# A graph network on one core: VectorE in a written-out order, neighbour lists by original node number, sorted slots weighted by ScalarE and summed in one instruction

## The chip, the cores and the metric

The kernel runs on one core of a Trainium2 chip. A core has five engines with a queue each: TensorE (PE; its weight loads are shown apart as PEld), VectorE (DVE), ScalarE (ACT), GpSimd (POOL) and SyncE (SP). Each works through its own instructions in order, and they wait for each other by semaphores. The metric is the device time of one execution in microseconds, the median of three runs. The profile comes from one further execution.

## The reference

There are B = 16 graphs ("entries") of N = 1024 nodes with C = 64 features, and an adjacency in which each node has a handful of neighbours. Four layers follow each other, each with a residual and a layer norm. Layers 2 and 3 do nearly all of the work here, and they are alike:

```python
x = _layernorm(x + _L0_gnn_ref(...))   # tanh MLP of [x, adj @ x]
x = _layernorm(x + _L1_gnn_ref(x, adj))  # (adj / row sums) @ x
x = _layernorm(x + _L2_gnn_ref(...))   # below
x = _layernorm(x + _L3_gnn_ref(...))   # below, with other weights
# layers 2 and 3:
nb = (adj_ > 0) & (~eye)[None]
skip = jnp.where(m > T_THRESH, (m + K_DIL - 1) // K_DIL, 1)
removed = nb & do_dil[..., None] & ((rank + 1) % skip[..., None] == 0)
rem = removed | jnp.swapaxes(removed, 1, 2)
vals = jnp.where(valid[..., None], x[:, None, :, :], big)
sv = jnp.sort(vals, axis=2)
q = gather(lo) * (1.0 - frac) + gather(hi) * frac
agg = agg + wt * q
h = jax.nn.relu(jnp.einsum('bnc,ch->bnh', x + agg, W1) + b1)
y = (jnp.einsum('bnh,ho->bno', h, W2) + b2) * mask[..., None]
```

In words: a node with more than ten neighbours loses every so many-th of them (and the loss is made symmetric). Then for each node and each feature the values of the remaining neighbours and of the node itself are sorted, and a weighted mean of the three quartiles is taken. A two-layer perceptron and a layer norm follow.

## The kernel before

For each entry there is a preparation and then two sorting phases, one for layer 2 ("layer 0" in the code's `quantiles`) and one for layer 3.

**Preparation** (`prepare`). The adjacency comes in by halves of 2 MB through a single buffer `adj_h`, twice: once for layer 0 (when `near`, the 0/1 matrix of neighbours, is taken from it) and once for layer 1. Then the lists are made. TensorE counts neighbours and their running ranks (`pr`, L458); ScalarE finds by two passes with Sign where a neighbour is to be dropped (L462); VectorE turns the places into one-hot rows `takes` (L470, two per tile of 128 rows); TensorE subtracts these and their transposes from `near` (`pv`, L479 to L485), and ScalarE keeps the rest as `left` (L486). The remaining neighbours are counted by TensorE (`pm`, L496), and the nodes are sorted by that count (keys, L497 to L508). `order` (L515) is the permutation matrix, and `down` (L516) the same, scaled by the place. TensorE permutes node data (`ps`, `px`) and the matrix of neighbours, once on each side: `pw` (L556, copied to `part`, L558) and `pk` (L567). VectorE's MAX8 and MATCH_REPLACE8 (L591, L593) read each row's neighbours out of `pk` as row numbers `idx`, by new, sorted node numbers. The features in the new order go to a DRAM table.

Sorted by count, the eight tiles of 128 nodes have 10, 11, 13, 14, 15, 17, 19 and 33 slots at most (`SIZES`).

**Sorting phase** (`quantiles`, one per entry and layer, 32 in all). Tiles are done from the largest down. For the seven smaller ones GpSimd copies the node's own row into slot 0 (L622) and issues one indirect DMA per further slot (L399, 92 gathers per phase, 128 rows of 256 bytes each) into one of four buffers `got`. For the largest tile, VectorE makes a one-hot matrix `hot` per slot (L630) and TensorE picks the rows with 24 matmuls (L395, features split in three bf16 parts); ScalarE copies eight slots at a time (L636). A sorting network of min and max instructions on VectorE (L639, 288 instructions per phase) moves the values between `got` and a second buffer `other`; only the exchanges that the wanted slots need are there. Then VectorE adds up the wanted slots, each times a weight per node (L644 for the first, L646 for each further one: seven slots for most tiles, 21 for the largest). The perceptron `mlp` ends the phase. For the first of the two layers the result is split in three bf16 parts and written to the table of the second; for the last, GpSimd scatters the rows to the output by `out_rows` (L657).

**What sets the order.** `weave` takes steps in turn from the sorting phases of entry k (layer 0) and k - 1 (layer 1) and from the preparation of entry k + 1, by the share of steps done. The framework's scheduler then orders each engine's instructions, VectorE's among them, and each engine keeps that order. GpSimd's gathers wait for a free `got` buffer, that is, for VectorE's last read of the tile that had it; SP's loads of the adjacency wait for `adj_h`. A general path at the end, for graphs with more neighbours than `SIZES` allows, is skipped in these runs.

Of the kernel before, what the change touches and what calls it, by code (L numbers as in the profile page):

```python
# [126 lines left out]
def exchange_plan(n, want, width=60):  # L127
# [50 lines left out]
    at, (_, ops) = min(beam.items(), key=lambda item: item[1][0])  # L178
    return ops, at
# [3 lines left out]
def adj_resnorm_kernel(ctx: ExitStack, tc: tile.TileContext, x, adj_t, nodemask, w01, b01, w02, b02,  # L183
# [7 lines left out]
    s = SimpleNamespace()  # L191

# [8 lines left out]
    minus_b = const.tile([P, P], BF, name="minus_b")  # L201
    nc.vector.tensor_scalar(minus_b, ident, -1.0, None, op0=ALU.mult)
# [11 lines left out]
                   allow_small_or_imprecise_dtypes=True)  # L214
    eps = const.tile([P, 1], F32, name="eps")
# [49 lines left out]
    table = [[dram.tile([N + 1, C], F32, name=f"table{layer}{i}") for i in range(2)] for layer in range(2)]  # L265
# [18 lines left out]
    def layernorm(dst, y):  # L284
        st = s.work.tile([P, 4, NT], F32, name="ln_st")
        nc.vector.reduce_sum(st[:, 0], y, axis=AX.X)
        nc.vector.tensor_scalar(st[:, 1], st[:, 0], 1.0 / C, None, op0=ALU.mult)
        nc.vector.tensor_sub(y, y, st[:, 1, :, None].to_broadcast([P, NT, C]))
        sq = s.work.tile([P, NT, C], F32, name="ln_sq", bufs=1)
        nc.scalar.activation(sq, y, AF.Square)  # L290
        nc.vector.reduce_sum(st[:, 2], sq, axis=AX.X)
        nc.scalar.activation(st[:, 3], st[:, 2], AF.Sqrt, bias=eps, scale=1.0 / C)
        nc.vector.reciprocal(st[:, 0], st[:, 3])
        nc.vector.tensor_mul(dst, y, st[:, 0, :, None].to_broadcast([P, NT, C]))

    def transposed(src, name):

        dst = s.work.tile([C, N], F32, name=name, bufs=1)
# [22 lines left out]
    def layer0(adj_half, x_s, x1):  # L321
# [3 lines left out]
        for h in range(NH):  # L325
            cols = slice(h * HALF, (h + 1) * HALF)
            adj_h = adj_half(h, True)
# [7 lines left out]
            nc.scalar.activation(hid_t[:, cols], ph[:C], AF.Tanh, bias=b01c)  # L335
        pd = s.psum.tile([P, NT, C], F32, name="pd", tag="mm", bufs=4)
        for t in range(NT):
            nc.tensor.matmul(pd[:, t, :], hid_t[:, t * P : (t + 1) * P], w02s, start=True, stop=True)
        y = s.work.tile([P, NT, C], F32, name="y")
        nc.vector.tensor_add(y, pd, x_s)  # L340
        nc.vector.tensor_add(y, y, b02r[:, None, :].to_broadcast([P, NT, C]))
        nc.vector.memset(x1[:, :, C : C + 1], 1.0)
        layernorm(x1[:, :, :C], y)

    def layer1(adj_half, x1, x2):
        y = s.work.tile([P, NT, C], F32, name="y")
        G = NT // 2
        for g in range(2):
            adj_h = adj_half(g, False)
            pa = s.psum.tile([P, G, C + 1], F32, name="pa", tag="mm", bufs=4)  # L350
            for q in range(G):
                for jt in range(NT):
                    nc.tensor.matmul(pa[:, q, :], adj_h[:, jt, q * P : (q + 1) * P], x1[:, jt, :],  # L353
                                     start=jt == 0, stop=jt == NT - 1)
            deg = s.work.tile([P, 2, G], F32, name="deg")
            nc.vector.tensor_scalar(deg[:, 0], pa[:, :, C], 1.0, None, op0=ALU.max)
            nc.vector.reciprocal(deg[:, 1], deg[:, 0])
            nc.vector.tensor_mul(y[:, g * G : (g + 1) * G, :], pa[:, :, :C],
                                 deg[:, 1, :, None].to_broadcast([P, G, C]))
        nc.vector.tensor_add(y, y, x1[:, :, :C])  # L360
        layernorm(x2, y)

    def mlp(xc, agg, mask, weights, dst):
        w1s, b1c, w2s, b2r = weights
        y = s.work.tile([P, NT, C], F32, name="y")
        nc.vector.tensor_add(agg, agg, xc)  # L366
        o_t = transposed(agg, "x_t")
# [9 lines left out]
        nc.vector.tensor_add(y, pd, b2r[:, None, :].to_broadcast([P, NT, C]))  # L377
        nc.vector.tensor_mul(y, y, mask[:, :, None].to_broadcast([P, NT, C]))
        nc.vector.tensor_add(y, y, xc)
        layernorm(dst, y)  # L380

    def split(xc, parts):

        rest = s.work.tile([P, NT, C], F32, name="rest", tag="y")
        nc.scalar.copy(parts[:, :, 0, :], xc)
        nc.vector.tensor_sub(rest, xc, parts[:, :, 0, :])
        nc.scalar.copy(parts[:, :, 1, :], rest)
        nc.vector.tensor_sub(rest, rest, parts[:, :, 1, :])
# [16 lines left out]
    def prepare(b, e):  # L405


# [4 lines left out]
        def adj_half(h, first):  # L412

            adj_h = s.feat.tile([P, NT, HALF], F32, name="adj_h", bufs=1)
            cols = slice(h * HALF, (h + 1) * HALF)
            load_adj(b, adj_h, cols)
            if first:
                nc.vector.tensor_scalar(near[:, :, cols], adj_h, 0.0, None, op0=ALU.is_gt)
            return adj_h

        x1 = s.feat.tile([P, NT, C + 1], F32, name="x1", bufs=1)
        x2 = s.feat.tile([P, NT, C], F32, name="x2", bufs=1)
        layer0(adj_half, x_s, x1)
        flat = near.rearrange("p t n -> p (t n)")
        diag = flat[:, : (NT - 1) * (N + P)].rearrange("p (t n) -> p t n", n=N + P)[:, :, :P]
        nc.vector.tensor_mul(diag, diag, off_diag[:, None, :].to_broadcast([P, NT - 1, P]))
        nc.vector.tensor_mul(flat[:, NT * N - P :], flat[:, NT * N - P :], off_diag)
        yield
        layer1(adj_half, x1, x2)
        x2p = s.feat.tile([P, NT, 3, C], BF, name="x2p", bufs=1)  # L430
        split(x2, x2p)
        yield


        st = s.work.tile([P, 6, NT], F32, name="nb_st", bufs=1)
        half = s.work.tile([P, NT], I32, name="nb_half", bufs=1)
        m, dil, lim, cut_at, gone = st[:, 0], st[:, 1], st[:, 2:4], st[:, 4:6], st[:, 4:6]
# [15 lines left out]
        for t in range(NT):  # L453
# [10 lines left out]
            if t % 2:  # L464
                yield
# [433 lines left out]
```

## Time and profile before

| | |
|---|---|
| time, median of 3 runs | 7654.07 us (7639.69 to 7656.64) |
| profiled execution | 7622.83 us, its span 7621.1 us |
| mean granted TensorE clock | 0.717 |
| GpSimd gathers L399 | 2944, 3098.5 us |
| VectorE exchanges L639 | 9216 in 8 groups, 3642.5 us |
| VectorE weighting L644 and L646 | 2240, 604.7 us |
| TensorE picks for the largest tile L395, `pgk` | 24576 matmuls, 1056.9 us |
| TensorE second permutation L556, `pw` | 2048 matmuls, 468.4 us |

Busy time is the time in which at least one instruction of the group ran, so a group's figure can be less than its count times its mean. The idle time of an engine is put down to what ended it: a producer by line, "remote" for something that the trace does not show on this core, "issue" where nothing that the trace shows was waited for. The windows give, for a stretch of time, the busy us of PE, PEld, DVE, ACT and POOL with the number of instructions in brackets, then the granted TensorE clock, the mean share of the DMA engines and GB/s.

### The profile page before, as it was taken

To read this page: it belongs to the slowest core of one execution; us is meant where nothing else is said; L and a number is where in the kernel's file an instruction comes from. 1 tells how busy PE (TensorE), PEld (TensorE's weight loads), DVE (VectorE), ACT (ScalarE), POOL (GpSimd) and SP (SyncE) were. 2 spreads that over 40 slices of the span, in tenths; PEclk is the share of its full clock that TensorE was granted. 3 is DMA by queue.
4 is the path that set the end of the run, shared out by engine and by line. 5 is a ranking of instruction groups with operands and counts; after the bars stand their busy time and mean duration, and the time that the engine had idled before them with its cause. 6 is when DMAs were issued, how large, how long until landed. Compare 5 with 4: busy or idle time off the path is not lost.

```text
span 7621.1 us, 112178 instructions
## 1 busy us (share of the span) xinstructions
PE 4154.8 (55%) x44488; PEld 2599.1 (34%) x44488; DVE 5224.3 (69%) x15234; ACT 1125.1 (15%) x1728; POOL 3354.9 (44%) x3338
## 2 busy tenths in 40 slices
PE   7565645456464565645556554565645566554122
PEld 4333323234342333424234331433423343332111
DVE  2567667767667696666777667696666876667666
ACT  3021102011020211102011020111202011020000
POOL 0333354543445444453543445344454444544543
PEclk8787767777676777767777667777766777767555
DMA  1202011020201102011020201102011020100000
GB/s 62 59 15 58 15 41 38 16 59 14 62 18 36 40 16 60 17 41 38 16 60 14 61 18 30 46 15 60 18 40 39 15 59 16 50 18 15 18 17 10
DMA packets 224020, 255.27 MB, mean 33 GB/s; under 512 B 108650, under 2 KB 108794, under 8 KB 223482
## 3 DMA queue, kind: packets, MB, share of 16 engines
q0 software_dynamic: 98304, 100.86, 7.0%
q1 hardware_dynamic: 125178, 147.13, 6.2%
q8 instruction: 350, 5.73, 0.3%
q14 instruction: 188, 1.54, 0.1%
HBM read 235.18 MB, written 12.58 MB: 33 GB/s over the span
## 4 chain that ended last, share of the span: by engine, by line
DVE 37%; PE 20%; another core or an unknown queue 19%; issue 9%; ACT 4%; DMA 1%; POOL 1%; SPq 0%; DVEq 0%; POOLq 0%; ACTq 0%
DVE got L639 11%; DVE other L639 10%; PE pgk L395 6%; DVE agg L646 3%; DVE best L591 3%; PE pa L353 3%; DVE hot L630 3%; PE pr L458 2%; DVE less L593 2%; PE pg L330 2%; ACT junk L506 1%; PE pv L482 1%; DMA adj_h<-in_adj_dram 1%; ACT junk L462 1%
## 5 line engine op out<-in xcount | busy, mean ns | idle before, releaser
L399 POOL DMA_INDIRECT got<-table,idx x2944 | 3098.5, 1052 | 983.3 <-issue 885.8
L395 PEld LDWEIGHTS <-hot 128*128 128x128 bf16 x24576 | 894.9, 103 | 558.5 <-issue 445.3
L639 DVE TENSOR_TENSOR other<-got 128x256 f32<-128x256 f32 (+9 forms) x2176 | 896.9, 425 | 71.2 <-issue 17.9
L622 POOL COPY got<-x2s 128x64 f32<-128x64 f32 x128 | 39.9, 315 | 2039.2 <-DVE agg L646 1611.0
L639 DVE TENSOR_TENSOR got<-other 128x256 f32<-128x256 f32 (+8 forms) x1792 | 736.2, 421 | 27.3 <-remote 7.9
L630 DVE TENSOR_SCALAR hot<-place 128x1024 bf16<-128x1024 f16 x1024 | 431.4, 423 | 449.4 <-remote 273.2
L639 DVE TENSOR_TENSOR got<-got 128x64 f32<-128x64 f32 (+8 forms) x1600 | 656.6, 414 | 33.4 <-DVE agg L646 14.0
L395 PE MATMUL pgk<-x2sp,hot 128*128 128x64 bf16 x12288 | 535.8, 203 | 242.7 <-issue 211.1
L567 PE MATMUL pk<-part,order 128*128 128x512 f16 x2048 | 518.4, 413 | 254.6 <-DVE less L593 221.8
L395 PE MATMUL pgk<-x3sp,hot 128*128 128x64 bf16 x12288 | 521.1, 201 | 181.0 <-issue 150.1
L458 PE MATMUL pr<-steps,near 128*128 128x512 bf16 x1536 | 397.9, 417 | 360.0 <-ACT junk L462 359.8
L302 PE MATMUL pt<-ident,agg 128*64 128x128 f32 x256 | 59.4, 411 | 955.0 <-DVE agg L366 913.9
L622 POOL COPY got<-x3s 128x64 f32<-128x64 f32 x128 | 71.9, 568 | 1072.7 <-DVE agg L646 834.5
L556 PE MATMUL pw<-down,left 128*128 128x512 f16 x2048 | 468.4, 387 | 24.6 <-DVE down L516 24.4
L646 DVE SCALAR_TENSOR_TENSOR agg<-got,wts,agg 128x64 f32<-128x64 f32 x1568 | 422.3, 277 | 69.0 <-remote 23.4
L497 DVE TENSOR_SCALAR own<-pm 128x8 f16<-128x8 f32 x16 | 2.8, 173 | 626.7 <-PE pm L496 626.7
L639 DVE TENSOR_TENSOR other<-other 128x64 f32<-128x64 f32 (+9 forms) x1024 | 390.8, 385 | 24.0 <-DVE got L639 7.1
L567 PEld LDWEIGHTS <-order 128*128 128x128 bf16 x2048 | 208.2, 105 | 556.6 <-DVE less L593 255.1
L482 PEld LDWEIGHTS <-takes 128*128 128x128 bf16 x2048 | 169.6, 113 | 631.0 <-issue 519.5
L302 PEld LDWEIGHTS pt<-ident,agg 128*64 128x64 f32 x256 | 39.1, 165 | 974.8 <-DVE agg L366 561.1
L303 ACT COPY x_t<-pt 64x512 f32<-64x512 f32 x96 | 54.1, 585 | 2111.3 <-issue 1152.0
L458 PEld LDWEIGHTS <-near 128*128 128x128 bf16 x1536 | 163.2, 109 | 552.2 <-issue 415.0
(184 smaller groups left out, 6950.9 us busy)
## 6 DMA issues: line engine op xcount, KB each, us to landing
adj_h<-in_adj_dram SPq DMA_DIRECT2D x512, 256.0 KB
got<-table,idx POOLq DMA_INDIRECT x2944
x_s<-in_x_dram SPq DMA_DIRECT2D x16, 256.0 KB
table<-x2s SPq DMA_DIRECT2D x16, 256.0 KB
table<-x3s SPq DMA_DIRECT2D x16, 256.0 KB
out_dram<-x4s,out_rows POOLq DMA_INDIRECT x128
table<-no_row SPq DMA_DIRECT2D x4, 0.2 KB
b02r<-in_L_gnn_b_dram SPq DMA_DIRECT2D x1, 32.0 KB
```

The costliest lines, as they stand in the source:

```text
L330: nc.tensor.matmul(pg[:C], x_s[:, jt, :], adj_h[:, jt, :], start=jt == 0, stop=jt == NT - 1)
L353: nc.tensor.matmul(pa[:, q, :], adj_h[:, jt, q * P : (q + 1) * P], x1[:, jt, :], start=jt == 0, stop=jt == NT - 1)
L395: nc.tensor.matmul(dst, hot[:, c, :], parts[:, c, q, :], start=first and c + q == 0, stop=c == NT - 1 and q == 2)
L399: nc.gpsimd.indirect_dma_start(out=dst, out_offset=None, in_=tab, in_offset=bass.IndirectOffsetOnAxis(ap=rows, axis=0))
L458: nc.tensor.matmul(pr[:, h * HALF : (h + 1) * HALF], near[:, c, t * P : (t + 1) * P], steps[:, N - P + h * HALF - c * P :][:, :HALF], star ...
L482: nc.tensor.matmul(pv[:, it * P : (it + 1) * P], takes[i][:, it, jt * P : (jt + 1) * P], minus_b, start=False, stop=False)
L556: nc.tensor.matmul(pw[:, cols], left[:, c, t * P : (t + 1) * P], down[:, c, cols], start=c == 0, stop=c == NT - 1)
L567: nc.tensor.matmul(pk[:, cols], order[:, c, t * P : (t + 1) * P], part[:, c, cols], start=c == 0, stop=c == NT - 1)
L591: nc.vector.max(best[:, k : k + 8], rest)
L630: nc.vector.tensor_scalar(hot, e.place, float(k), None, op0=ALU.is_equal)
L639: nc.vector.tensor_tensor(cut(pair[to], v, d if is_max else 0), cut(pair[a], v), cut(pair[b_], v, d), op=ALU.max if is_max else ALU.min)
L646: nc.vector.scalar_tensor_tensor(agg[:, t, :], value, wt, agg[:, t, :], op0=ALU.mult, op1=ALU.add)
```

## The change

VectorE's order is no longer the scheduler's. All its instructions of the main part are issued through `dve`, a wrapper that adds up an estimated duration for each (0.13 us and 960 elements per us, four times as many for some 16-bit instructions), and `manual_schedule` keeps them as written. The other engines stay with the scheduler. Every piece of work is a generator that yields a number of microseconds before its next VectorE instruction; the class `Weave` keeps a due time for each by the clock of `dve`. The sorting network of a phase is the base: after each of its instructions `catch_up` steps all pieces that are due.

The work itself changes in these places:

- Slots: ScalarE multiplies each wanted slot by its weight into `prods` (2240 instructions), and VectorE sums them by one `reduce_sum` per tile (256). The exchange plan is now the one with all wanted slots ending in `got`; it has 288 instructions per phase as before, with the same elements.
- The largest tile is filled one phase ahead (`fill`), in two buffers, its slots 3.3 us apart by the clock.
- Lists: `takes` is one tile in place of two, from |slot - mid| = off, with the absolute value on ScalarE; `left` carries N minus the original node number in place of 1, so that the product `order` times `left` gives the lists by original number, and `pw`, `part` and `down` go. Counting what is left moves from TensorE (`pm`) to ScalarE (a Sign pass with a sum).
- Tables are in the original order, three per layer. The first result `x2` goes there directly; the second one is scattered by GpSimd with `rows`, eight indirect DMAs per entry, read back by SP as `x3` and split from there. One of three splits goes.
- Buffers: `y`, the layer norm's statistics and some others are named per chain; `junk` has three buffers, `wts`, `idx` and `none` four, `rows`, `out_rows` and `mask` five.

Where the pieces stand, by the instruction order of VectorE: in a phase one `hot` stands after every 5 to 9 exchanges, the eight `takes` after every 2 to 5, and the seven MAX8 groups of an entry between the last tiles of a phase, the last three of them next to each other.

```diff
+class Metered:
...
+            self.us += 0.13 + size / (3840 if fast else 960)
...
-        nc.vector.tensor_scalar(gone, cut_at, float(N), 0.5, op0=ALU.add, op1=ALU.mult)
-        takes = [s.sets.tile([P, NT, N], BF, name=f"takes{i}", tag=f"set{i + 1}") for i in range(2)]
...
+            if t < NT:
+                dists.append(s.work.tile([P, N], F16, name="dist", tag="junk", bufs=3))
+                nc.scalar.activation(dists[t], slot, AF.Abs, bias=mid[:, t : t + 1])
+            yield 1.5
+            if t >= 2:
+                dve.tensor_scalar(takes[:, t - 2, :], dists[t - 2], off[:, t - 2 : t - 1], None, op0=ALU.is_equal)
...
+                nc.tensor.matmul(pv[:, cols], near[:, c, rows], scaled[:, c, :], start=True, stop=False)
+                nc.tensor.matmul(pv[:, cols], takes[:, c, rows], minus_n, start=False, stop=False)
+                nc.tensor.matmul(pv[:, cols], minus_n, takes[:, t, cols], start=False, stop=True)
+            nc.scalar.activation(left[:, t, :], pv, AF.Relu)
...
-                    nc.tensor.matmul(pw[:, cols], left[:, c, t * P : (t + 1) * P], down[:, c, cols],
-                                     start=c == 0, stop=c == NT - 1)
-            nc.scalar.copy(part[:, t, :], pw)
...
+                dve.tensor_scalar(hot, e.place, float(k), None, op0=ALU.is_equal)
...
+                pick(pg[:, k - g, :], hot, e.parts[layer], whole)
+                yield 3.3
...
+        for i, k in enumerate(want):
+            nc.scalar.activation(prods[:, i, :], got[:, k, :], AF.Copy, scale=e.wts[:, t, k : k + 1])
+        yield 9
+        dve.reduce_sum(agg[:, t, :], prods.rearrange("p k c -> p c k"), axis=AX.X)
...
+        dst, rows = (out_rows_of, e.out_rows) if layer else (table[1][b % 3], e.rows)
...
+            nc.sync.dma_start(x3, dst[:N, :].rearrange("(t p) c -> p t c", p=P))
...
-            for i, k in enumerate(wants[t]):
-                value, wt = pair[at[k]][:, k, :], e.wts[:, t, k : k + 1]
-                if i == 0:
-                    nc.vector.tensor_scalar(agg[:, t, :], value, wt, None, op0=ALU.mult)
-                else:
-                    nc.vector.scalar_tensor_tensor(agg[:, t, :], value, wt, agg[:, t, :], op0=ALU.mult, op1=ALU.add)
...
+            for is_max, d, v, a, b_, to in usual[t]:
+                dve.tensor_tensor(cut(pair[to], v, d if is_max else 0), cut(pair[a], v), cut(pair[b_], v, d),
+                                  op=ALU.max if is_max else ALU.min)
+                yield
+            yield weigh(e, t, got, agg)
...
+        def catch_up(self):
+            while self.works:
+                work = min(self.works, key=lambda w: w[0])
+                if work[0] > self.now():
+                    return
+                self.step(work)
...
+        main.enter_context(tc.manual_schedule(engines={mybir.EngineType.DVE}))
...
+            for new in sort_tiles(b, entries[b], layer, agg):
+                if new:
+                    weave.add(new)
+                weave.catch_up()
+            finishing[b, layer] = weave.add(finish(b, entries[b], layer, agg))
...
+            phase(k, 0, (k - 1, 1))
+            phase(k - 1, 1, (k + 1, 0))
```

A phase first finishes its own fill, then whatever the fill of the following phase needs (the preparation of entry k + 1, or the end of the first layer), starts that fill, and then sorts. Preparations start one after another: that of entry b + 1 when the lists of entry b are made.

## The prediction

> **What bounds the kernel now.** I read the totals of the page first, then what VectorE (DVE) waited for, then the span in windows of 12 and 15 us, then the costliest groups. Totals:
>
> ```profile
> PE 4154.8 (55%) x44488; PEld 2599.1 (34%) x44488; DVE 5224.3 (69%) x15234; ACT 1125.1 (15%) x1728; POOL 3354.9 (44%) x3338
> ```
>
> VectorE is the busiest, and 7621.1 - 5224.3 = 2397 us of the span it stands idle. POOL's figure leaves out the gap after each gather, so the group list is needed:
>
> ```profile
> L399 POOL DMA_INDIRECT got<-table,idx x2944 | 3098.5, 1052 | 983.3 <-issue 885.8
> L622 POOL COPY got<-x2s 128x64 f32<-128x64 f32 x128 | 39.9, 315 | 2039.2 <-DVE agg L646 1611.0
> L646 DVE SCALAR_TENSOR_TENSOR agg<-got,wts,agg 128x64 f32<-128x64 f32 x1568 | 422.3, 277 | 69.0 <-remote 23.4
> ```
>
> A gather holds POOL (3098.5 + 885.8) / 2944 = 1.353 us. There are 32 sorting phases (16 entries, two layers), 92 gathers each. POOL otherwise waits for VectorE to free a gather buffer. So VectorE's work and its idle time set the pace. Its waits, with total, count and longest:
>
> ```profile
> DVE own L497 <- PE pm L496: 626.7, 15, 44.5
> DVE hot L630 <- remote: 273.2, 56, 28.7
> DVE y L377 <- remote: 221.2, 10, 32.7
> DVE hot L630 <- PE pgk L395: 174.7, 125, 8.6
> DVE deg L356 <- PE pa L353: 124.3, 32, 15.2
> ```
>
> Once per entry it stands some 42 us before L497 for TensorE sums that take 1.6 us. The windows tell why (busy us, then instructions, for PE, weight loads, DVE, ACT, POOL):
>
> ```profile
> 3515.00:3527.00 12.00, 6.27 (x48) 3.79 (x46) 11.20 (x39) 1.72 (x2) 9.40 (x11) 0.86 0.16 24
> 3527.00:3539.00 12.00, 2.23 (x8) 0.50 (x8) 1.08 (x5) 0.00 (x0) 9.26 (x10) 0.64 0.13 27
> 3539.00:3551.00 12.00, 3.79 (x17) 1.95 (x17) 0.00 (x0) 1.02 (x1) 9.09 (x12) 0.64 0.17 25
> 3551.00:3563.00 12.00, 1.97 (x5) 0.52 (x5) 0.00 (x0) 0.00 (x0) 6.40 (x7) 0.50 0.11 22
> 3563.00:3575.00 12.00, 7.36 (x94) 5.47 (x93) 3.13 (x14) 3.19 (x4) 0.00 (x0) 0.64 0.00 1
> ```
>
> While gathers run without a break, TensorE falls to single matmuls; the moment they stop, all engines run. It is no data wait, for in the last stage, where VectorE only sorts, the same happens to it:
>
> ```profile
> 7320.00:7335.00 15.00, 0.00 (x0) 0.00 (x0) 14.88 (x55) 0.00 (x0) 11.26 (x10) 0.50 0.10 17
> 7335.00:7350.00 15.00, 0.00 (x0) 0.00 (x0) 14.14 (x45) 0.00 (x0) 10.67 (x13) 0.50 0.11 22
> 7350.00:7365.00 15.00, 0.00 (x0) 0.00 (x0) 13.51 (x49) 0.00 (x0) 11.79 (x13) 0.50 0.13 26
> 7365.00:7380.00 15.00, 0.00 (x0) 0.00 (x0) 5.54 (x19) 0.00 (x0) 11.47 (x14) 0.50 0.17 26
> 7380.00:7395.00 15.00, 0.00 (x0) 0.00 (x0) 4.02 (x13) 0.00 (x0) 11.47 (x14) 0.50 0.14 25
> 7395.00:7410.00 15.00, 0.00 (x0) 0.00 (x0) 3.13 (x10) 0.00 (x0) 11.34 (x13) 0.50 0.14 25
> ```
>
> For 45 us of a burst of gathers it keeps its pace (149 instructions), then drops to 12.7 busy us in 45, a share of 0.28. I read this as instructions that arrive too slowly beside the gathers:
>
> ```profile
> q8 instruction: 350, 5.73, 0.3%
> q14 instruction: 188, 1.54, 0.1%
> ```
>
> [...]
>
> **Idle time by kind.** Waits put down to nothing local, or to TensorE while it crawled (626.7, 273.2, 221.2, and 102.5 + 54.3 + 47.0 + 43.0 + 25.9 from the same list): 1394 us, 43.6 per phase. Plain waits for a producer (174.7, 124.3, and 117.9 for the adjacency, 60.9 and 59.1, 38.2, 35.8, 25.1, 19.1): 655 us, 20.5 per phase. The other 348 us are start, end and crumbs.
>
> **VectorE's work.** Weighting goes: L646 1984 instructions, 422.3 + 117.1 us, and L644 256, 65.3 us, together 604.7. In their place stand 256 sums: 224 over about 7 slots of 64 (448 elements) and 32 over 21 slots (1344). The nearest row, L291, sums 512 elements in 0.681 us; by element 0.60 and 1.79 us, 134 + 57 = 191 us. It reads unit steps and the new sums read with a stride; at half speed they would cost 382. I take 191, as the adds that read strided blocks of `got` (L639) show no slower rate: 128x256 advances in 0.34 us in the timeline, about 960 elements per us after 0.07. Half of `takes` goes (L470, 102.7): 51.3. `down` goes (L516): 69.2. One of three splits goes (10.9 + 11.0): 21.9. Small copies moved to ACT (9 us) pay for new small instructions. The sorting networks keep their 288 instructions and all their elements. Sum: 5224.3 - 604.7 + 191 - 51.3 - 69.2 - 21.9 = 4668 us, 146 per phase.
>
> **The other engines.** POOL keeps 2944 gathers (3984 us) and 256 copies (112) and gets 128 more scatters, since the layer's result is now written by row indices: 256 x (1.103 busy, L657, + 0.3 issue) = 359. Sum 4455 us, 139 per phase: 7 us below VectorE, so no phase can fall much under 146. Gather indices in the original order change no count. ACT gets 2240 scalings of 128x64: between 0.301 us (128x8, L292) and 0.585 (64x512, L303); I take 0.33, nearer the small one: 739 us. With 128 `dist` (1.11) and 128 counting passes (1.31), less `part` (129.5), and one split less (30), it comes to some 2.0 ms, under a third; at 0.585 to 2.6 ms. Seven scalings add 2.3 us between a tile's last exchange and its buffer's release, covered by the three other buffers; uncovered, 224 x 2.3 = 515 us, inside the high end below. In ACT's queue some stand behind copies that wait for TensorE, so a late TensorE now holds gather buffers too. TensorE loses `pw` (468.4) and L496 (31.2), and 3072 small `pv` matmuls at L482's 0.122 us replace 568: about 3460 us, 108 per phase, not the bound. The read-back of `x3` through SP stands before the next adjacency loads, and behind scatters; its user, the second layer's fill, begins a whole phase later. If that cover went, the chain costs about the 12 us that its yield stands for, 16 times: 192 us.
>
> **Idle after.** The laid-down order puts one `hot` between 5 to 9 exchanges and the list pieces between tiles, so a producer's latency mostly lies behind sorting. Of the plain 20.5 us per phase I keep half, 10; bounds 0 and 20.5. For the fetch stall, follow POOL's order: three tiles per phase (12, 10 and 9 gathers) are gathered one by one as a buffer comes free, 12 to 16 us each, too short to hurt. But the three lightest tiles are sorted in 7 to 10 us each by the row's rates (3840 to 5632 elements), quicker than the next phase's 18, 16, 14 and 13 gathers arrive. These 61 run in one burst of 61 x 1.353 = 83 us. VectorE has 45 us at full pace and 38 at 0.28: it loses 38 x 0.72 = 27, say 28 with its copies. Bounds: 0 (the breaks fall so that every burst stays under 45 us) and today's 43.6. Idle: 348 + 32 x (28 + 10) = 1564.
>
> **Sum.** 4668 + 1564 = 6232 us of span. The profiled execution took 7622.8 with a span of 7621.1, and the median is 7654.1, so 33 us are added: 6265 us.
>
> [...]
>
> **Rivals.**
> - Short bursts (chance 0.20, below 5820). [...] Idle 348 + 32 x 10 = 668, time 4668 + 668 + 33 = 5369. For it: the windows keep full pace for 45 us. Against: POOL has 139 of 146 us to work and can hardly pause.
> - The stalls stay (0.17, 6710 to 7640). The order was laid by a clock that knows nothing of fetching, so the idle time of a phase keeps its 64 us: 4668 + 348 + 32 x 64 + 33 = 7097. For it: a fixed queue stops at its first late piece, and `hot` has only three buffers. Against: VectorE was in order before as well.
> - Slower (0.07). Gathers and VectorE take turns: TensorE serves about 200 matmuls of a burst (201 in the 48 us up to 3527), a hot tile needs 24, every exchange behind it waits, and only 45 us per phase overlap. Then a phase lasts 139 + 146 - 45 = 240 us, idle 94: 4668 + 348 + 3008 + 33 = 8057. It turns into a loss from 81 us idle per phase ((7654 - 33 - 5016) / 32). Against: today's idle is 64 with half the gathers already under sorting.
>
> **How the numbers follow.** The forecast (0.55) holds from 24 to 52 us idle per phase, 5817 to 6713. No difference has 0.01. The range takes the first rival and most of the second: 5400 to 6950, with about 0.2 outside. Under 0.2% this kernel's measurement tells nothing. Faster is 0.55 + 0.20 + 0.17 = 0.92, same 0.01, slower 0.07.
>
> **What would show it.** Right: VectorE busy 4.6 to 4.75 ms, the sums 0.6 and 1.8 us each, ACT near 2.0 ms, no 40 us wait at the `own` line, and windows in which TensorE drops to a few matmuls once per phase near its boundary, ending with the burst. Wrong: POOL busy without pause while TensorE runs at full pace (first rival), or VectorE idle over 60 us per phase, at `hot` above all (second). Strided sums of 1.2 us would add 191 us.

## The result, and the profile after

The changed kernel is slower: 7936.2 us (median of 4, 7925.0 to 7941.3) against 7655.4 us (median of 4), a ratio of 1.0368 with a 95% interval of 1.035 to 1.0387. I had forecast 6265 us. The totals of the profiled execution, span 7934.8 us:

```profile
PE 3952.0 (50%) x41672; PEld 2657.4 (33%) x41672; DVE 5239.9 (66%) x12971; ACT 1806.0 (23%) x4256; POOL 3289.3 (41%) x3466
```

VectorE runs 2263 instructions fewer and is busy 15.6 us longer (5224.3 before), and it stands idle 7934.8 - 5239.9 = 2695 us (2397 before). Both halves of my sum failed. What it waits for (engine, line, releaser: us in total, times, longest):

```profile
DVE hot L196 <- remote: 621.4, 85, 27.0
DVE hot L196 <- PE pgk L431: 474.8, 142, 15.2
DVE best L196 <- remote: 363.5, 19, 39.4
DVE agg L196 <- ACT prods L694: 227.9, 16, 25.3
```

The 626.7 us at `own` are gone. In their place VectorE waits 1096 us at `hot`, 34 us in a phase, and 364 us at the list pieces, 19 times for 19 us on average: pieces that now have a fixed place in its row and whose matmuls are late.

The new sums, out of the costliest groups:

```profile
L196 DVE TENSOR_REDUCE agg<-prods 128x64 f32<-128x448 f32 (+2 forms) x224 | 203.4, 908 | 228.1 <-ACT prods L694 227.9
```

0.908 us for 448 elements where I took 0.60. The windows (columns as in the prediction's) show a burst of gathers and its end:

```profile
3732.00:3744.00 12.00, 0.00 (x0) 0.00 (x0) 11.19 (x34) 2.41 (x10) 9.03 (x10) 0.54 0.13 25
3744.00:3756.00 12.00, 5.71 (x16) 1.99 (x16) 11.53 (x20) 1.26 (x5) 9.31 (x11) 0.75 0.17 26
3756.00:3768.00 12.00, 5.31 (x16) 1.92 (x16) 5.76 (x16) 0.35 (x1) 9.25 (x11) 0.68 0.14 26
3768.00:3780.00 12.00, 0.00 (x0) 0.00 (x0) 3.58 (x8) 2.00 (x7) 9.10 (x11) 0.50 0.17 25
3780.00:3792.00 12.00, 5.54 (x16) 1.97 (x16) 1.61 (x2) 0.00 (x0) 9.39 (x11) 0.78 0.16 27
3792.00:3804.00 12.00, 0.00 (x0) 0.00 (x0) 0.00 (x0) 0.00 (x0) 7.58 (x9) 0.50 0.15 25
```

The gathers have run without a gap of 2.5 us since 3724.7; VectorE is down to half its pace 31 us later, not 45. TensorE's 16 matmuls at a time are the sums of the next list piece. They take 5 to 6 us once they start, but they start only when VectorE has made `less`, and the list piece after them starts only when the gathers have ended (at 3802.0), for a reason that the trace does not show:

```profile
3780.29 5.54 PE L608 MATMUL pk<-left,order 128*128 128x512 f16 x16 [18.84 <-DVE less L196]
3806.87 1.23 DVE L196 MAX8 best<-pk 128x8 f32<-128x1024 f32 x1 [24.96 <-remote]
```

Why busy time did not fall is seen in the step from one instruction to the next. Before, from VectorE's timeline (start, duration):

```profile
3470.80 0.68 DVE L294 TENSOR_TENSOR x<-y,ln_st 128x512 f32<-128x512 f32 x1
3471.40 0.88 DVE L639 TENSOR_TENSOR got<-got 128x704 f32<-128x704 f32 x1
3472.20 0.68 DVE L386 TENSOR_TENSOR rest<-x,x2p 128x512 f32<-128x512 f32 x1
3472.80 0.81 DVE L639 TENSOR_TENSOR got<-other,got 128x640 f32<-128x640 f32 x1
```

and after:

```profile
3629.66 0.69 DVE L196 TENSOR_TENSOR other<-got 128x512 f32<-128x512 f32 x1
3630.39 0.69 DVE L196 TENSOR_TENSOR got<-got 128x512 f32<-128x512 f32 x1
3631.00 0.35 DVE L196 TENSOR_TENSOR got<-other 128x192 f32<-128x192 f32 x1
3631.38 0.36 DVE L196 TENSOR_TENSOR other<-other 128x192 f32<-128x192 f32 x1
```

Before, pieces of other work stand between the exchanges, and each instruction starts 0.08 us before the one ahead of it ends (0.60 us after a start of 0.68). After, the maximum at 3630.39 overwrites what the minimum before it reads, and starts 0.04 us after its end: 0.73 us instead of 0.61. Counted over all neighbours in VectorE's trace (its bookkeeping records included, which puts busy 9 to 28 us above the page's figure; an overlap is counted from 20 ns up, and the pairs in the fourth row have a gap between them):

```
                                 before   after   e1     e8     e13
sum of durations, us             6274     5901    5828   5880   5878
pairs that overlap               12351    6872    12042  8630   9574
their overlap, us                1186     794     1231   927    1027
gaps of 20 to 150 ns             3060     6421    1252   4535   3577
busy (union), us                 5252     5257    4760   5097   5017
```

So 373 us of durations went away and 392 us of overlap with them. The columns e1, e8 and e13 belong to the experiments.

### The profile page after: what moved, and what is told of

It is laid out like the page before. It is cut to its first block, busy times and chain, and to the rows that moved or that the text cites. A ratio compares the mean times of both kernels' runs of the same rounds, so it can differ in the third digit from the quotient of the medians.

```text
span 7934.8 us, 107638 instructions
## 1 busy us (share of the span) xinstructions
PE 3952.0 (50%) x41672; PEld 2657.4 (33%) x41672; DVE 5239.9 (66%) x12971; ACT 1806.0 (23%) x4256; POOL 3289.3 (41%) x3466
## 5 line engine op out<-in xcount | busy, mean ns | idle before, releaser
L435 POOL DMA_INDIRECT got<-table,idx x2944 | 2930.9, 996 | 922.4 <-issue 895.7
L431 PEld LDWEIGHTS <-hot 128*128 128x128 bf16 x24576 | 1103.3, 113 | 2049.3 <-issue 884.7
L431 PE MATMUL pgk<-x3p,hot 128*128 128x64 bf16 x12288 | 709.7, 223 | 1118.5 <-issue 461.8
L608 PE MATMUL pk<-left,order 128*128 128x512 f16 x2048 | 656.6, 478 | 821.9 <-DVE less L196 607.2
L196 DVE TENSOR_TENSOR other<-got 128x256 f32<-128x256 f32 (+10 forms) x2080 | 875.6, 435 | 80.1 <-ACT got L683 13.4
L431 PE MATMUL pgk<-x2p,hot 128*128 128x64 bf16 x12288 | 590.1, 208 | 670.6 <-DVE hot L196 362.1
L694 ACT ACTIVATE prods<-got,wts 128x64 f32<-128x64 f32 x1568 | 408.1, 337 | 1485.6 <-issue 822.9
L196 DVE TENSOR_TENSOR got<-got 128x256 f32<-128x256 f32 (+6 forms) x1472 | 635.3, 434 | 98.4 <-remote 30.6
L536 PE MATMUL pv<-scaled,near 128*128 128x128 f16 x1024 | 270.6, 279 | 307.6 <-issue 207.0
L537 PE MATMUL pv<-minus_n,takes 128*128 128x128 bf16 x1024 | 272.0, 280 | 228.6 <-DVE takes L196 119.9
L507 ACT ACTIVATE junk<-pr,nb_st 128x1024 bf16<-128x1024 f32 x256 | 282.5, 1109 | 446.1 <-PE pr L503 169.3
```

What stands on the lines that cost most here:

```text
L196: return call(*args, **kwargs)
L431: nc.tensor.matmul(dst, hot[:, c, :], parts[:, c, q, :], start=first and c + q == 0, stop=c == NT - 1 and q == 2)
L435: nc.gpsimd.indirect_dma_start(out=dst, out_offset=None, in_=tab, in_offset=bass.IndirectOffsetOnAxis(ap=rows, axis=0))
L507: nc.scalar.activation(junk, pr, AF.Sign, bias=lim[:, i, t : t + 1], scale=-1.0, accum_out=cut_at[:, i, t : t + 1])
L536: nc.tensor.matmul(pv[:, cols], near[:, c, rows], scaled[:, c, :], start=True, stop=False)
L537: nc.tensor.matmul(pv[:, cols], takes[:, c, rows], minus_n, start=False, stop=False)
```

## The experiments

The kernel before took 7644 to 7656 us beside the first two groups of runs (e1 to e5; e7 to e9 and m1) and 7756 to 7767 us beside the other two (e10 to e12 and m2; e13), 1.5% more. Ratios are to the kernel before of the same group; a time in us is compared only inside a group.

**e1: the order left to the scheduler.** One line of the changed kernel is taken out:

```
-        main.enter_context(tc.manual_schedule(engines={mybir.EngineType.DVE}))
```

> The changed kernel with only the laid-down order of VectorE taken back: the scheduler orders VectorE again, lists, weighting by ScalarE and the sum in one go stay. Order theory (the fixed order sets dependent instructions next to each other, so each starts after the end of the one before it instead of 0.1 us earlier): VectorE's busy time falls from 5240 us to 4850 or less, the pairs that overlap rise from 6872 to over 9500, time near 7500. Fetch theory (long bursts of gathers keep instructions from arriving, whatever the order): busy time may fall, but the idle time takes it up, time 7700 to 8000. Third view (the order does what it was written for, and it is the list or weighting part that costs): without it the time is over 8000.

7004.4 us, ratio 0.9168 (0.9152 to 0.9183). Its totals:

```profile
span 6946.2 us, 107593 instructions
...
PE 3768.7 (54%) x41672; PEld 2562.4 (37%) x41672; DVE 4750.6 (68%) x12971; ACT 1806.1 (26%) x4256; POOL 3694.5 (53%) x3466
```

The same 12971 instructions cost VectorE 489 us less (4750.6 against 5239.9), with 12042 overlapping pairs, and it is idle 2196 us instead of 2695. The laid-down order alone costs 13% of the time (1.0368 / 0.9168), some 920 us by the medians and 988 by the two profiled executions (that of e1 was the quickest of its five); without it the change is a gain of 8%. The third view fell, and so did the fetch theory's 7700 to 8000; the order theory's 7500 was too careful: as much again comes from idle time. VectorE's idle time before the list pieces (`best`) is 99 us in all where it was 454, and before `hot` 970 where it was 1134.

**e3 and e9: the weighting alone.** e3 is the kernel before with ScalarE's scalings and one sum; they are packed in place in `got`, for want of memory. e9 is e1 with VectorE's weighting put back.

```
# e3                                        # e9
+prods = got[:, : len(want), :]             -nc.scalar.activation(prods[:, i, :], ...)
+nc.scalar.activation(prods[:, i, :], ...)  -dve.reduce_sum(agg[:, t, :], ...)
+nc.vector.reduce_sum(agg[:, t, :], ...)    +dve.scalar_tensor_tensor(agg[:, t, :], value, wt, ...)
```

> The kernel before with the weighting alone changed: exchanges end in the gathered tile, ScalarE scales the wanted slots (packed in place), VectorE sums them in one instruction. My prediction's step: VectorE loses 604.7 us and gains the sums, busy 5224 to about 4900, time about 7300 if idle time stays. Order theory: the weightings stood between dependent exchanges and cost only their step of 0.20 us each, 2240 x 0.2 = 450, less sums of 281, so busy falls by 170 or less, and time by no more than 170 (7480 to 7650). If the hand-over to ScalarE is itself a loss: over 7700.

> The changed kernel with VectorE's order left to the scheduler and the slots weighted by VectorE again (no products on ScalarE, no sums). Only the lists by original numbers and what goes with them (x3 scattered, TensorE's orders, copies on ScalarE) then differ from before. If the weighting by ScalarE is worth its 170 us of busy time: about 7170. If it costs more in waits (326 us at the sums) than it saves, as it did alone in the kernel before: under 6950. By my prediction's own price for the weighting it would be over 7400.

e3: 7777.8 us, ratio 1.0178 (1.016 to 1.0197). VectorE's busy time falls from 5224 to 5039.9, by 184 us, but its idle time rises by 333 us: new waits come in (166 us at the sums for ScalarE, 307 us at `nb_st` for ScalarE's counting passes or for nothing named), while `own` loses 300. So the weighting alone makes the kernel before slower, by less than 2%. e9: 7084.0 us, ratio 0.926 (0.9216 to 0.9303), busy 4903.3. Read against e1, the weighting is worth 153 us of busy time and 1% of the time (0.926 to 0.9168, intervals that do not touch). My price for it was 414 us. The weightings took 0.277 us each, but their step was 0.20, and where exchanges depend on one another they stood in a place that is now empty. e9 also says what the rest is worth: 7.4% for the lists by original numbers, the largest tile filled a phase ahead, the tables and the buffers together, which no run tells apart.

**e8 and e13: the laid-down order with fewer dependent neighbours.** In e8 the exchanges of a tile are put in another valid order, in e13 the heaviest tile's exchanges also alternate with those of the lighter tiles.

```
-    usual = [exchange_plan(k, want) for k, want in zip(SIZES, wants)]
+    usual = [spread(exchange_plan(k, want)) for k, want in zip(SIZES, wants)]
# e13 besides
+        streams = [exchanges([NT - 1]), exchanges(reversed(range(NT - 1)))]
+            for stream in list(streams):
+                    yield next(stream)
```

> The changed kernel, laid-down order kept, but the exchanges inside each tile are put in another order, so that as few as the network allows read or overwrite what the one before them touched: by the plan 99 such neighbours in 288 exchanges a phase instead of 168. Order theory: 69 x 32 = 2208 pairs overlap again at about 0.12 us each, VectorE's busy time falls by some 200 to 265 us from 5240, and the time by as much if the idle time stays, 7680 to 7740. If the lost overlap is not what made VectorE's busy time stay: busy over 5180.

> The laid-down order kept, exchanges spread as in the run e8, and besides the heaviest tile's 66 exchanges alternate one by one with the first 66 of the lighter tiles, which touch other buffers. By the plan some 58 neighbours of 288 in a phase then depend on each other, against 99 in e8 and 168 in the changed kernel. If adjacency is what took the overlap: VectorE's busy time falls below e8's 5097 (union) to about 4950 to 5000, overlapped pairs over 9500; the time by as much where the idle time stays, about 7600 to 7750 on the chip of the first runs. If something else in the laid-down order keeps VectorE busy: 5080 or more.

```profile
span 7849.7 us, 107652 instructions
...
PE 3884.7 (49%) x41672; PEld 2624.2 (33%) x41672; DVE 5079.3 (65%) x12971; ACT 1817.0 (23%) x4256; POOL 3277.6 (42%) x3466
```

That is e8: 7828.7 us, ratio 1.0216 (1.018 to 1.0252). Busy falls by 161 us, idle rises by 75, so the time stays over the 7740 that I expected at most. 1758 pairs more overlap; 161 / 1758 is 0.09 us each, under the 0.12 that I took. e13:

```profile
span 7473.8 us, 107533 instructions
...
PE 3800.1 (51%) x41564; PEld 2567.2 (34%) x41672; DVE 4998.0 (67%) x12971; ACT 1800.2 (24%) x4256; POOL 3525.2 (47%) x3466
```

7451.9 us, ratio 0.9594 (0.9569 to 0.962): still a laid-down order, with the exchanges alone (and with them the start of the lighter tiles' gathers) in another place, 4% faster than before. Busy is 242 us under the changed kernel's; with the bookkeeping records it is 5017 us, 17 over the range that I gave, and 9574 pairs overlap. From the changed kernel over e8 and e13 to e1, busy time falls with each step in the number of overlapping pairs. Two stages of the small kernels below have the pair by itself, without gathers, both with maxima of 128x256 on VectorE (it is the third engine of the first line, stage n of m2, and the first of the second, stage a of m1):

```profile
2010.00:2040.00 30.00, 0.00 (x0) 0.00 (x0) 27.76 (x66) 0.00 (x0) 0.00 (x0) 0.50 0.00 0
30.00:60.00 30.00, 30.00 (x91) 0.00 (x0) 1.00 0.00 0
```

Where each maximum overwrites what the one before it made, 66 start in 30 us, one in 0.46 us; where none depends on its neighbour 91 do, one in 0.335 us. The granted clock differs, but it is TensorE's, and at 1900 to 1930 us, with 0.92 granted, VectorE's figures in n are the same 27.76 (x66). So it is shown that neighbours that depend on each other took the overlap. In e13 the time fell by more than the busy time; two rows of work also leave a late piece more cover, but that was not tried by itself.

**e7 and e10: half the gathers.** Every second slot is filled by a copy from the slot beside it, so other rows are sorted; in the scheduler's order (e7) and in the laid-down one (e10).

```
-                for k in range(1, size):
+                for k in range(1, size, 2):
                     gather(got[:, k, :], tab, e.idx[:, t, k - 1 : k])
+                nc.gpsimd.tensor_copy(got[:, 2 : 2 * n + 1 : 2, :], got[:, 1 : 2 * n : 2, :])
```

> The changed kernel with VectorE's order left to the scheduler, and every second gather left out (its slot is filled by a copy on GpSimd from the slot beside it, so other rows are sorted): 1472 fewer gathers, some 2 ms less of GpSimd. All the other work is the same. Fetch theory: VectorE's idle time falls from 2196 us to 1300 or less, time under 6250. If the idle time is plain latency between engines (TensorE too slow at its granted clock, hand-overs with ScalarE): idle stays over 1900, time over 6650.

> The changed kernel, laid-down order kept, with every second gather left out and its slot filled by a copy on GpSimd, as in the run with half the gathers in the scheduler's order (5558 us, 770 us of idle on VectorE). If the laid-down order costs only the overlap of dependent instructions: busy 5250, idle near 790, time near 6050. If its fixed places cost waits of their own, gathers or not: idle over 1200, time over 6450. In both cases the idle time beyond that (2695 now) is the gathers'.

The totals of e7, then of e10:

```profile
span 5556.1 us, 106804 instructions
...
PE 3475.2 (63%) x41672; PEld 2450.2 (44%) x41672; DVE 4765.5 (86%) x12971; ACT 1802.8 (32%) x4256; POOL 2428.3 (44%) x2250
```

```profile
span 6130.2 us, 106766 instructions
...
PE 3682.8 (60%) x41575; PEld 2586.4 (42%) x41672; DVE 5256.4 (86%) x12971; ACT 1810.4 (30%) x4256; POOL 2049.8 (33%) x2250
```

5557.8 us and 6131.9 us, one run each. 1504 gathers are left, so 1440 are gone and not the 1472 of the expectation. VectorE's idle time is 791 us in e7 and 874 in e10, where it was 2196 and 2695. So 1440 gathers fewer take away 1405 us of idle time in the one order, 0.98 us for each gather, and 1821 us in the other. With half the gathers the laid-down order costs its 491 us of busy time (5256.4 - 4765.5) and 83 us of idle time beside, though e10 ran in the slower group; with all of them it costs 499 us of idle time more. Plain latency between the engines is not what VectorE waits for, nor are the gathered rows: its exchanges stood 13.6 us for them in e1. What shrinks from e1 to e7 is the waiting for the other engines, before `hot` from 970 to 260 us and before the sums from 326 to 24.

**m1 and m2: a burst by itself.** Two kernels that leave the whole computation out: in each stage one engine has a straight row of instructions that need nothing from the others, beside 200 gathers.

```
for k in range(gathers):
    nc.gpsimd.indirect_dma_start(out=got[:, k, :], in_=x_rows, in_offset=...)
for k in range(act):
    nc.scalar.activation(acts[k % 4][:, :64], go[:, :64], AF.Copy, scale=2.0)
...
```

> A kernel that leaves the whole computation out. In seven stages, one after the other, VectorE runs a straight row of independent maxima while GpSimd runs 200 gathers of 128 rows of 64 in one go: a 600 of 256 elements without gathers, b and g 600 of 256 with them, c 200 of 1024, f 1200 of 64, d as b with a 4 us break on GpSimd after every 10 gathers, e as b with a 16 us break after every 40. Fetch theory: a runs at 0.34 us an instruction throughout; in b, c, f and g VectorE keeps its pace for about the same number of instructions (100 to 300), whatever their length, which is 35 to 100 us in b and over 100 us in c and under 40 us in f, and then falls under a share of 0.4, with no or few 16 KB packets on q8 until the gathers stop. Rival, contention for memory or ports: every instruction is longer under gathers, from the first on, and the share of time lost is alike for all widths. Breaks: if 4 us let a block in, d keeps a share over 0.7; if only long ones do, e does and d does not.

> A kernel that leaves the whole computation out; seven stages again, with 200 gathers each except n. h: 600 sums of 256 elements on VectorE (one input); i: 900 scalings of 64 elements on ScalarE; j: 1500 matmuls of 64 columns, each with its weight load, on TensorE; k: 500 maxima of 256 elements on VectorE, each overwriting the one before; l: 1000 independent maxima of 64 elements; n: k, i and j together without gathers; o: the three together with gathers. Instruction theory (beside gathers the instructions themselves arrive late, on every engine): in h, i, j and l the engine falls, after the instructions it had, to one in 0.7 to 1.4 us, and back when the gathers stop; o far longer than n. [...]

ScalarE in stage i of m2 (its five columns of engines are as before, ScalarE the fourth, GpSimd the fifth):

```profile
412.00:422.00 10.00, 0.00 (x0) 0.00 (x0) 0.70 (x5) 9.40 (x65) 7.30 (x8) 1.00 0.08 23
422.00:432.00 10.00, 0.00 (x0) 0.00 (x0) 0.00 (x0) 4.93 (x30) 7.56 (x9) 1.00 0.10 27
432.00:442.00 10.00, 0.00 (x0) 0.00 (x0) 0.00 (x0) 2.63 (x12) 7.56 (x9) 1.00 0.09 26
632.00:642.00 10.00, 0.00 (x0) 0.00 (x0) 0.00 (x0) 1.79 (x7) 7.61 (x7) 1.00 0.08 23
702.00:712.00 10.00, 0.00 (x0) 0.00 (x0) 0.00 (x0) 10.00 (x70) 0.00 (x0) 1.00 0.00 0
```

65 scalings in the first 10 us, then 30, 12, and 7 for as long as the gathers run; 70 again when they have stopped. TensorE in stage j, from the timeline:

```profile
900.80 0.21 PE L55 MATMUL ps<-go_b_j 128*128 128x64 bf16 x1 [2.59 <-issue]
902.20 0.11 PEld L55 LDWEIGHTS <-go_b_j 128*128 128x128 bf16 x1 [2.69 <-issue]
903.60 0.21 PE L55 MATMUL ps<-go_b_j 128*128 128x64 bf16 x1 [2.59 <-issue]
905.00 0.11 PEld L55 LDWEIGHTS <-go_b_j 128*128 128x128 bf16 x1 [2.69 <-issue]
```

One instruction every 1.40 us, a weight load and a matmul in turn, at a granted clock of 1.00 and with nothing to wait for. VectorE does the same in h (sums, 7 in 10 us), in k (dependent maxima) and in f of m1 (7 in 10 us); and with three engines at work at once (o) each has its own 7 instructions in 10 us. Before that each engine kept a faster pace: for some 77 sums, 95 scalings, 92 matmuls with their loads, 182 dependent maxima, in 16 to 85 us, counted until two steps in a row were over 1 us. DMA engines were busy a tenth of the time (0.08 to 0.10). So the slow pace that the instruction theory forecast came about on all three engines; the granted clock was 1.00 in h, i and j, and no row of the slow stretches of i and j names another engine that was waited for.

But the reason that I gave, that instructions come late, is not shown by j. When TensorE ran alone at full pace, from 1063 to 1104 us, packets of 16 KB came on q8, one in 3.7 us, and none on q14. From 797 to 1063 us, while the gathers ran and TensorE crawled, the queues carried this:

```profile
q0 software_dynamic: 6075, 6.23, 8.4%
q14 instruction: 2, 0.02, 0.0%
```

Two packets on q14 and not one on q8, and from 804 to 1063 TensorE started 98 matmuls and 99 loads, at its slow pace. Then it ran 53 of each in 3 us, from before the next packet began (1064.3 us):

```profile
1063.22 2.98 PE L55 MATMUL ps<-go_b_j 128*128 128x64 bf16 x53 [0.49 <-issue]
1063.24 2.86 PEld L55 LDWEIGHTS <-go_b_j 128*128 128x128 bf16 x53 [0.60 <-issue]
```

So TensorE's slow 259 us went without a packet on q8, and its pace came back before the next one; what held its instructions up, no run shows. The slow stretch was of one length beside 200 gathers: from the start of the first of the 200 to the end of the last slow step it lasted 277 to 281 us in h, i, j, k and o alike, 1.40 us for each gather, though the gathers themselves were issued within 253 us in h, i and j (1.27 us apart) and within 276 and 278 us in k and o.

In m1, stage b, and in l of m2 it went the other way round: 600 and 1000 independent maxima of two inputs ran at full pace, and one gather lasted as long as they did (202 and 135 us). It did not in c and f of m1, which have independent maxima too: no gather took over 2.0 and 2.8 us there. What decides it is not shown. In b:

```profile
221.84 202.00 POOL L43 DMA_INDIRECT got<-in_x_dram,rows_b  x1 [220.87 <-DVE rows_b L37]
424.14 0.94 POOL L43 DMA_INDIRECT got<-in_x_dram,rows_b  x1 [0.30 <-issue]
```

In the full kernels this hardly shows: a gather takes 0.996 us on average after the change, and 0.94 in b once the maxima were done. My expectation that b and g would fall like the others was wrong for this reason, and the stages d and e were spoiled by it, so that breaks could not be read from m1.

**e4, e5 and e12: breaks between the gathers.** Small iotas on GpSimd, free of dependencies in e4 (changed kernel) and e5 (kernel before), tied to the tile's slots in e12 (on e1).

```
+        if done[0] % 8 == 0:                               # e4, e5
+            for _ in range(5):
+                nc.gpsimd.iota(idle, ...)
+                for _ in range(5):                         # e12
+                    nc.gpsimd.iota(got[:, 1:size, :], ...)
```

> The changed kernel, with five small iota instructions on GpSimd (about 3 us in all) before every eighth gather; 368 pauses, 1.1 ms of GpSimd time, nothing else changed. Fetch theory, if a short break lets the blocks of instructions in: q8 packets inside bursts rise from 105 to over 200, VectorE's idle time falls from 2695 by 500 or more, time under 7450. If the engines starve by the sheer share of gathers and not by their being unbroken, or if the supply of gathered rows is the limit: time 7900 to 8500.

> The kernel before with the same pauses (twelve smaller iotas, about 3 us, before every eighth gather). Fetch theory with short breaks enough: the windows in which VectorE falls to a share of 0.1 to 0.4 after 40 us of a burst go, idle time falls from 2397 by 500 or more, time under 7150. Otherwise 7650 to 8200.

> The changed kernel in the scheduler's order (7004 us) with a break ahead of each tile's gathers: five iotas on GpSimd, about 4 to 5 us, that write the tile's slots, so that they stand between two tiles' gathers and cannot be put ahead of all; 224 breaks, 1.0 ms. This is the trial of breaks that the two earlier runs missed, since their iotas were all put ahead of the first gather. If breaks of 4 to 5 us in a burst let the other engines catch up: VectorE's idle time falls from 2196 by 300 or more, time under 6750. If each gather costs its share whatever stands between: time 6950 to 7250.

e4 8041.8 us, ratio 1.0516 (1.0499 to 1.0534); e5 8065.3 us, ratio 1.0547 (1.0526 to 1.0567). Both tell nothing of breaks: the scheduler put the iotas in some 45 and 50 clumps in the first 2.1 and 2.8 ms, and none later (not all ahead of the first gather, as the expectation of e12 says). In e12 they stand where they should. Bursts of over 40 us, counted as gathers and scatters less than 2.5 us apart, fall from 41 to 4; yet the time is 7170.5 us, ratio 0.9248 (0.9214 to 0.9282) against 0.9168. VectorE's idle time is 2336 us where it was 2196. Its share in the first 10 us of a burst is 0.74 where it was 0.86, and in the next 10 us of those that last 20 it is 0.62 where it was 0.94. Breaks of 4 to 5 us do not help. With the 1.40 us per gather of m2 this points to the number of gathers and not to how long they run unbroken; longer breaks were not tried. In m2 the last slow step ended 24 to 27 us after the last gather where one engine worked alone (h, i, j), and 2 to 3 us after it in k and o.

**e11: a copy out of GpSimd's row.** After the change GpSimd stood 845 us before one copy in the row of the gathers, waiting for ScalarE.

```
-        nc.gpsimd.tensor_copy(got[:, 0, :], e.xs[layer][:, t, :])
+        nc.scalar.copy(got[:, 0, :], e.xs[layer][:, t, :])
```

> The changed kernel with one copy moved: the first slot of the heaviest tile is copied by ScalarE instead of GpSimd, where it stood in the row with the gathers and waited 845 us for ScalarE. Queue theory (what stands in GpSimd's row before the gathers makes them late and bunches them): VectorE's idle time falls by 200 us or more, time under 7740. If those waits of GpSimd cost nothing: 7880 to 7980.

8069.2 us, ratio 1.039 (1.0355 to 1.0424), no other than the changed kernel's 1.0368. The wait moved to the next copies in the row (`got` for ScalarE's products, 1303 to 2053 us). That copy's place in the row is not what bunches the gathers; since the wait only moved, the run does not say what GpSimd's waiting for ScalarE costs. The scatters of x3 and of the output, which wait 988 us in the same row, were not moved by themselves.

## Why the prediction was wrong

It put VectorE's span at 4668 busy and 1564 idle; measured are 5240 and 2695, 572 and 1131 us more. By the runs the 572 are 489 for the order (e1) and 261 for a weighting priced too high (e9), less 179 for lists that saved more than I counted. The 1131 are 499 for the order and 632 for stalls that were there without it (e1).

1. **The step that failed: "The sorting networks keep their 288 instructions and all their elements."** The count and the elements did stay, but the sum took from this that their time stays too: it put the order at nothing, without a reason. I had taken the exchanges at the rate of an order in which a scheduler had filled the places between dependent ones with other work. The laid-down order put them side by side, 168 of 288 in a phase, and each such pair costs some 0.1 us (0.09 in e8, 0.12 in the small kernels): 489 of the 572 us (e1), and e8 and e13 give parts of it back. I had read in the timeline that "128x256 advances in 0.34 us" and did not ask what made it 0.34 and not the 0.46 of dependent neighbours.
2. **"so a producer's latency mostly lies behind sorting"**: wrong beside gathers. The order costs 499 us of idle time with all gathers and 83 with half of them (e1, e7, e10). A fixed row stops at a `hot` or a list piece whose matmuls are late; the scheduler's row stops there less, by 164 and 354 us.
3. **Stall by burst length, 28 us per phase, 10 for plain waits.** This term failed too. Right was that beside gathers TensorE, VectorE and ScalarE are slow, one instruction in 1.40 us in m2, and that the rows of i and j name no other engine that they waited for. The reason that I read into it was not shown: in j TensorE was slow for 259 us without a packet on q8, and ran 53 matmuls in 3 us before the next one. The form was wrong: I gave each burst 45 us free and thought of shorter bursts as free, which no run shows; after the change VectorE was at half its pace after 31 us, in m2 the faster pace held for 77 to 182 instructions, in 16 to 85 us, each gather of m2 went with 1.40 us of slow stretch, and breaks of 4 to 5 us give nothing back (e12). Without the laid-down order idle time is 2196 us: less the 348 of the start, end and crumbs, 58 us per phase where I had 38, so 632 us more. The second rival, "the stalls stay", had 64 and 7097 us; e1 took 7004.
4. **The weighting, 604.7 - 191.** Measured 153 to 184 us (e9, e3). I subtracted durations (0.277 us) where the steps (0.20) count, and the strided sum takes 0.908 and 2.41 us, 281 in all; the small one lies midway between the 0.60 that I took and the 1.2 that I had named as a bound, and the large one is nearer to my 1.79 than to twice that. On the other side the lists and what goes with them took 321 us off VectorE's busy time (5224.3 to 4903.3 in e9), where I had 142; some 196 of them are durations, the rest is more overlap.
5. **What held:** no long wait at `own` any more; ScalarE 1.81 ms for 2.0; GpSimd 131 us per phase with 896 us between gathers counted ((3289.3 + 895.7) / 32) for 139. TensorE was busy 3952 us for my 3460, at a mean granted clock of 0.655 (0.717 before).
6. **The rival on the other side**, gathers and VectorE taking turns with a phase of 240 us, came nearest: with its own 348 us apart a phase lasts (7934.8 - 348) / 32 = 237 us. That is in part luck. One half of it was right, that a gather costs VectorE about its own time (0.98 us each in e7, where a gather takes 0.996 after the change), but its 94 us of idle per phase are 73, which makes up for a busy time taken for 4668. The sign that I had named against the forecast, over 60 us idle per phase at `hot` above all, came about.

e1 beats both kernels: 0.9168 of the time before. The list and weighting parts are worth keeping together, the laid-down order in this form is not.

## What to carry to other kernels

A duration in a profile is not a price. The price of an instruction is its step to the next start, and in these runs that depended on its neighbour (0.335 us for a 128x256 maximum beside an independent one, 0.46 us beside a dependent one): before a change takes work out of a row or fixes the order of one, count how many neighbours will read or overwrite each other's data. Where an engine falls behind on all sides at once while GpSimd gathers, count gathers and instructions: here a gather cost VectorE about 0.98 us, and halving them was worth a fifth of the time.

## What the runs showed of the hardware

Beside 200 indirect gathers in one row (m2) TensorE, VectorE and ScalarE each started one instruction in 1.40 us after a faster pace for 77 to 182 instructions, alone (h, i, j, k) and all three at once (o). From the first gather to the last slow step it was 277 to 281 us, 1.40 us for each gather issued, up to 27 us past the last one, and TensorE's slow 259 us in j went without a packet on q8. An independent row of two-input maxima on VectorE held one gather for 202 us in b of m1 (135 in l of m2, not in c and f of m1), while a row of dependent ones let them through 1.38 us apart in k (1.27 beside ScalarE alone, in i). Two neighbours that depend on each other started about 0.12 us later than two that do not (0.46 us in n of m2 and 0.335 us in a of m1, for 128x256); in the kernel before, independent neighbours overlapped by 0.08 us.
